# A four-layer selective-scan kernel: y, x and the projection moved in pieces, convolution and input projection in column pairs

## The chip, the cores and the metric

The kernel runs on one core of a Trainium2 chip. The metric is device time in microseconds. A core has TensorE (PE, matmuls, with its weight loads shown apart as PEld), VectorE (DVE), ScalarE (ACT), GpSimd (POOL) and SyncE (SP); each works through its own instructions in order, and semaphores tie them together. In this kernel SP issues every DMA, and sixteen DMA engines carry the data.

## What is computed

Input x is (8, 48, 48, 96): eight images of 48 x 48 positions with 96 channels. Four layers follow each other, each adding to x a two-dimensional selective scan of its group-normalised input. Layers 0 to 2 have dt ranks 6, 16 and 6; layer 3 (rank 6) writes its recurrence as a quotient of cumulative sums.

```python
# one layer; B = 8 images, L = 48*48 positions, Din = 192 channels, N = 16 states, K = 4 directions
xz = gn(x) @ in_proj_w.T
xc, z = split(xz)
u = silu(depthwise_conv3x3(xc) + conv_b)
xs = [rows, columns, rows reversed, columns reversed] of u
dts, Bs, Cs = split(einsum('bkdl,kcd->bkcl', xs, x_proj))
delta = softplus(dt_proj(dts) + dt_bias)
h[n] = exp(delta * A[n]) * h[n] + delta * u * Bs[n]        # along the L positions
y = sum over n of h[n] * Cs[n]  +  D * u                   # summed over the 4 directions
x = x + (layernorm(y) * silu(z)) @ out_proj_w.T
```

## The kernel before

**Tiling.** The eight images are four pairs; a pair (l, p) of layer l is worked through before the next. Its 2 x 192 channels make three tiles t of 128 partitions (tile 0 and 1 the first 128 channels of either image, tile 2 the last 64 of both). For each tile there are two phases ph (along rows, along columns) and two directions d. A position axis of 2304 is cut into three stretches of 768 (`SCANS`); one (t, ph, d, stretch) is a `Chunk` (L684) of 16 scan steps, so a pair has 36 chunks and 576 steps. Step n takes 64 of the tile's 128 channels (n even or odd) and two of the 16 states, one on either half of the partitions, so that it scans 128 x 768 values.

**A scan step.** `load` and `load_b` have SP fetch C (tile cb) and, for six of sixteen steps, B (tile bb), each as two DMAs that broadcast a row of xd in DRAM to 64 partitions (`fetch`, L718 to L729). For the other ten steps TensorE spreads B from the rows in `brow` into PSUM (L667). ScalarE makes the decay exp(delta*A) (L764), GpSimd multiplies bb by du (L741) or VectorE does with the PSUM copy (L794), VectorE scans (L798), GpSimd multiplies cb by the state (L807), and TensorE sums over states into the PSUM tile acc (L854), with 64-column weights, two matmuls side by side.

**The order of work.** `run` (L1170) writes the instructions of the layers out in one order that each engine keeps. Loads for a step are written `LOADS` = 3 steps ahead (B one more), decays 2 ahead, and the sum `LAG` = 2 steps behind. Beside each step stands one step of side work (`beside`, L1264): either of `ahead`, the `prologue` (L287) of the following pair, or of `behind`, the `epilogue` (L998) of the pair before. These are generators; a `yield` ends a step, `yield True` marks that a PSUM bank is held, and `Side(g, total)` carries the number of steps it is expected to have, by which `side_step` keeps the two in proportion. In layer 3, whose chunks are short (`Edge`), ten side steps go beside each scan step. The side work and the preparation of chunks share two PSUM banks (`bank`, L273).

**The prologue.** For each image b of the pair it brings x into SBUF (96 x 2304 fp32, 864 KB): in layer 0 by transposes, and then stores it to the DRAM tile xs (L364); later it loads it from there (L366). Statistics with bn_stats (L373), the group norm, and the input projection to a padded image (L404 for the first 128 channels, L413 for the last 64) follow. `convolve` (L302) sums nine shifted matmuls with diagonal weights into a bank for each of five row groups (`CHUNKS`, four of 480 positions and one of 384). Last come four projections of u (`x_projection`, L467), one for each phase and image: each fills the tile xt, 2*rank + 64 rows by 2304, stores it to xd in DRAM as one DMA (L492; 76 rows, 684 KB, at rank 6, and 96 rows, 864 KB, at rank 16), reads the B rows back (`parts_of`, L431, fetch at L437) and stores them in bf16 parts as xb. `later(i, ...)` places work at step i of a projection's list.

**The sum and the epilogue.** `collect` (L863) copies acc into y, and with a tile's last chunk stores all of y (128 x 2304 fp32, 1152 KB) to yd (L875). The epilogue loads x and y back in pieces of three rows (L1028, 108 KB; L1030, 216 KB), applies layer norm, gate and output projection, and stores the new x (L1104).

Of the kernel before, what the change touches and what calls it, by code (L numbers as in the profile page):

```python
# [49 lines left out]
P = 128  # L50
NB, H, W, DM = 8, 48, 48, 96
L = H * W
# [51 lines left out]
def ss2d_layers_kernel(ctx: ExitStack, tc: tile.TileContext, x_in, consts, weights, out):  # L104
# [178 lines left out]


    GATED, READY = "gated", "ready"

    def prologue(l, p, short=False, first=False):  # L287
        ly = layers[l]
# [13 lines left out]
        def convolve(pad, t):  # L302

            while place["tiles"] < t and not first:
                yield GATED
            u[t] = upool.tile([P, L], F32, name=f"u_{l}_{p}_{t}", tag="u")
            for c0, m in CHUNKS:
                r0, nr = c0 // W, m // W
                ps = bank()
                for j in range(9):  # L310
                    dy, dx = divmod(j, 3)
                    nc.tensor.matmul(  # L312
                        ps[:, :m],
                        ly.diag[:, int(t == 2), j, :],
                        pad[:, r0 + dy : r0 + dy + nr, dx : dx + W],
                        start=(j == 0),
                        stop=(j == 8),
                    )
                    yield True
                nc.scalar.activation(  # L320
                    u[t][:, c0 : c0 + m], ps[:, :m], AF.Identity, bias=ly.column(t, C_CONVB)
                )
                yield
            silu(u[t], u[t])
            yield
# [6 lines left out]
        for b in range(2):  # L332
            x = tmp.tile([DM, L], F32, name=f"x_{l}_{p}_{b}", tag="tmp")
            if l == 0:
                loaded = []

                def load(c0, m):
                    ld = sm2.tile([P, 4, DM], F32, name="ld", tag="ld")
                    nc.sync.dma_start(
                        ld[: m // 4],  # L340
                        x_in[2 * p + b, c0 : c0 + m, :].rearrange("(q j) c -> q j c", j=4),
                    )
                    loaded.append(ld)

                load(*CHUNKS[0])
                load(*CHUNKS[1])
                for _ in range(3):
                    yield
                for i, (c0, m) in enumerate(CHUNKS):
                    q, ld = m // 4, loaded[i]  # L350
                    ps = bank()
                    for j in range(4):
                        nc.tensor.transpose(
                            ps[0:DM, j * q : (j + 1) * q], ld[:q, j, :], ident[:q, :q]
                        )
                    yield True
                    nc.scalar.copy(
                        x[:, c0 : c0 + m].rearrange("c (q j) -> c j q", j=4),
                        ps[0:DM, :m].rearrange("c (j q) -> c j q", j=4),
                    )  # L360
                    if i + 2 < NCH:
                        load(*CHUNKS[i + 2])
                    yield
                nc.sync.dma_start(src[b], x)  # L364
            else:
                nc.sync.dma_start(x, src[b])  # L366
            for _ in range(4):
                yield


            st = sm1.tile([DM, NCH, 6], F32, name="st", tag="st")
            for i, (c0, m) in enumerate(CHUNKS):
                nc.vector.bn_stats(st[:, i, :], x[:, c0 : c0 + m])  # L373
                if i % 2 == 1:
                    yield
            mv = sm1.tile([DM, 2], F32, name="mv", tag="mv")
            nc.vector.bn_aggr(mv, st.rearrange("p a b -> p (a b)"))
            yield
            ps = bank()
            nc.tensor.matmul(ps[0:DM, 0:1], minus_group, mv[:, 0:1], start=True, stop=True)  # L380
            yield True
            mg = sm1.tile([DM, 1], F32, name="mg", tag="mg")
            nc.scalar.copy(mg, ps[0:DM, 0:1])
            dv = sm1.tile([DM, 1], F32, name="dv", tag="dv")
            nc.scalar.activation(dv, mv[:, 0:1], AF.Square, bias=mg)
            nc.scalar.activation(dv, dv, AF.Identity, bias=mv[:, 1:2])
            yield
            ps = bank()
            nc.tensor.matmul(ps[0:DM, 0:1], group_w, dv, start=True, stop=True)
            yield True  # L390
            scale, shift = gn[:, b, 0:1], gn[:, b, 1:2]
            nc.scalar.activation(scale, ps[0:DM, 0:1], AF.Ln, bias=gn_eps[0:DM])
            nc.scalar.activation(scale, scale, AF.Exp, scale=-0.5)
            nc.scalar.activation(shift, mg, AF.Copy, scale=scale)
            nc.scalar.activation(x, x, AF.Identity, bias=shift, scale=scale)
            yield

            pad = padded(f"pad_{l}_{p}_{b}")
            q0 = 64 * b
            for c0, m in CHUNKS:  # L400
                r0, nr = c0 // W, m // W
                rows = slice(1 + r0, 1 + r0 + nr)
                ps = bank()
                nc.tensor.matmul(  # L404
                    ps[:, :m], ly.inw[:, 0:P], x[:, c0 : c0 + m], start=True, stop=True
                )
                yield True
                nc.scalar.copy(
                    pad[:, rows, 1 : W + 1], ps[:, :m].rearrange("p (r w) -> p r w", w=W)
                )  # L410
                yield
                ps = bank()
                nc.tensor.matmul(  # L413
                    ps[q0 : q0 + 64, :m], ly.inw[:, P:DIN], x[:, c0 : c0 + m], start=True, stop=True
                )
                yield True
                nc.scalar.copy(
                    pad2[q0 : q0 + 64, rows, 1 : W + 1],
                    ps[q0 : q0 + 64, :m].rearrange("p (r w) -> p r w", w=W),
                )  # L420
                yield
            if not (first and b == 1):
                yield from convolve(pad, b)
# [43 lines left out]
        def x_projection(i, ph, b):  # L467

            o, got = 15 * i, {}

            def put(ps, c0, m):
                if "xt" not in got:
                    got["xt"] = tmp.tile([ly.nx, L], F32, name=f"xt_{l}_{p}_{ph}_{b}", tag="tmp")
                xt, r0, nr = got["xt"], c0 // W, m // W
                if ph == 0:
                    nc.scalar.copy(xt[:, c0 : c0 + m], ps[: ly.nx, :m])
                else:
                    nc.scalar.copy(
                        xt.rearrange("p (w h) -> p h w", h=H)[:, r0 : r0 + nr, :],
                        ps[: ly.nx, :m].rearrange("p (r w) -> p r w", w=W),  # L480
                    )

            def mul(half, c0, m):
                if half == 0:
                    got["ps"] = bank()
                project(got["ps"], ph, b, half, lambda z: z[:, c0 : c0 + m], slice(0, m))

            for j, (c0, m) in enumerate(CHUNKS):
                later(o + 3 * j, True, mul, 0, c0, m)
                later(o + 3 * j + 1, True, mul, 1, c0, m)  # L490
                later(o + 3 * j + 2, False, lambda *a: put(got["ps"], *a), c0, m)
            later(o + 15, False, lambda: nc.sync.dma_start(xd[ph, b], got["xt"]))  # L492
            row = 2 * ly.rank
            parts_of(
                o + 19, ph, b,
                lambda d: xd[ph, b, row + 2 * NS * d : row + 2 * NS * d + NS, :].rearrange(
                    "n (q m) -> (n q) m", q=4
                ),
                lambda d: xb[ph, b, :, d].rearrange("k n (q m) -> (n q) k m", q=4),
                4 * NS, L // 4,  # L500
            )
# [167 lines left out]
                start=True, stop=True,  # L669
            )  # L670

    late_act, late_sums = [], []

    def collected():
        some = bool(late_sums)
# [8 lines left out]
    class Chunk:  # L684
# [178 lines left out]
        def collect(self):  # L863
# [8 lines left out]
            if self.ph == self.d == 1 and self.last:  # L872
                if t == 0:
                    s["yd"] = dram.tile([3, P, L], F32, name=f"yd_{l}_{p}", tag="yd")
                nc.sync.dma_start(s["yd"][t], s["y", t])  # L875

    class Edge:

# [119 lines left out]
    def epilogue(l, p):  # L998
# [26 lines left out]
        def load(i):  # L1025
# [4 lines left out]
            nc.sync.dma_start(y, yd[:, :, at].rearrange("t p m -> p t m"))  # L1030
            loaded[i] = x, y

        load(0)
        for _ in range(3):
            yield
# [134 lines left out]
    def run(pairs, short):  # L1170
# [58 lines left out]
        for k, ((l, p, unit), c, n) in enumerate(todo):  # L1229
# [4 lines left out]
            per = NS // QUAD if l in short else NS  # L1234
            all_units = len(groups) * (per if l in short else len(SCANS) * per)
            place["tiles"] = 3 * unit // all_units
            if done:
                behind, done = Side(epilogue(*done), 195), None
            if unit == LAG and following:
                ahead = Side(begin(*following), 300)  # L1240
            if k == 0:
                coming_to = 1
                coming = prepare(chunks[coming_to])
# [158 lines left out]
```

## Time and profile before

| | us |
|---|---|
| median of 3 runs | 20514.42 |
| lowest, highest | 20494.02, 20516.52 |
| the profiled execution | 20509.65 |
| its span, first to last instruction | 20507.7 |

Engine busy shares are 84% for TensorE, 86% for VectorE, 79% for ScalarE and 87% for GpSimd. The TensorE clock granted was 0.904 on average. The DMA engines moved 4200 MB, at 217 to 229 GB/s in every full slice of layers 0 to 2, with a busy share near 0.88. Layers 0 to 2 fill the span from 205 us to about 18,565; layer 3 takes the last 1,940 us, in which TensorE is busy for 1,581 and GpSimd for 703.

The DMAs that matter here, from the page's list of issues and the list of DMAs:

| tensors | line | count | KB each |
|---|---|---|---|
| cb<-xd and bb<-xd, the scan's loads | L724 | 13952 and 5184 | 192 |
| brow<-xb | L749, L916 | 864 | 72 |
| yd<-y | L875, and L995 in layer 3 | 48 | 1152 |
| xd<-xt, rank 6 and rank 16 | L492 | 32 and 16 | 684 and 864 |
| x<-xs and xs<-x | L366, L364 | 24 and 8 | 864 |

A group's line gives line, engine, operation, output and inputs with shapes, the count, then busy time and mean duration in ns of one, then the idle time of the engine just before it and what ended most of it. In the timelines the idle time stands in brackets. "SPq" are the queue's own instructions.

### The profile page before, as it was taken

The numbers are of one execution on the slowest core, as the hardware profiler recorded it, in microseconds if no ns is written. First come the engines' busy times: TensorE is split into PE (matmuls) and PEld (weight loads), VectorE is DVE, ScalarE is ACT, GpSimd is POOL, SyncE is SP. The second block draws the span as 40 slices with busy tenths as digits, with TensorE's granted clock in tenths as the row PEclk, the third lists the DMA queues.
The fourth block names the chain that finished last, engine by engine and source line by source line (L and its number), as shares of the span: only waits on it lengthen the run. The fifth ranks groups of instructions, "written<-read, shape, count | busy, mean of one in ns | idle before, by whom it ended". The sixth has DMA issues, their size and how long they took to land. (4 is left out here: it accounts for less than half of the span.)

```text
span 20507.7 us, 304889 instructions
## 1 busy us (share of the span) xinstructions
PE 17283.2 (84%) x88322; PEld 7546.6 (37%) x88322; DVE 17656.0 (86%) x14161; ACT 16243.7 (79%) x30020; POOL 17768.2 (87%) x10121
## 2 busy tenths in 40 slices
PE   8888888888888888888888888888888888888886
PEld 2323333333333333333333333333333333335565
DVE  5999999999999999999999999989989989995543
ACT  5777887887887887887877887877877877877776
POOL 5999999999999999999999999999999999995432
PEclk8998998998998999998998999988988998999997
DMA  5888888888888888888888888888888888883221
GB/s 147 223 221 222 219 220 224 222 219 221 220 225 222 219 229 221 221 229 219 221 228 220 217 225 219 218 218 220 217 219 219 220 219 222 219 220 109 76 72 51
DMA packets 1963444, 4200.13 MB, mean 205 GB/s; under 512 B 369456, under 2 KB 720048, under 8 KB 1948592
## 3 DMA queue, kind: packets, MB, share of 16 engines
q1 hardware_dynamic: 1961776, 4180.52, 77.8%
q8 instruction: 726, 11.89, 0.3%
q14 instruction: 942, 7.72, 0.2%
HBM read 4026.64 MB, written 152.27 MB: 204 GB/s over the span
## 5 line engine op out<-in xcount | busy, mean ns | idle before, releaser
L807 POOL TENSOR_TENSOR cb<-cb,da 128x768 f32<-128x768 f32 x4320 | 7831.3, 1817 | 799.5 <-issue 258.3
L854 PE MATMUL acc<-cb,twin 128*64 128x384 f32 x27648 | 7018.1, 542 | 663.6 <-POOL cb L807 660.3
L798 DVE TENSOR_TENSOR_SCAN da<-da,carry,b 128x768 f32<-128x768 f32 x2880 | 5223.3, 1814 | 176.4 <-ACT b L764 2.3
L741 POOL TENSOR_TENSOR bb<-bb,du 128x768 f32<-128x768 f32 x2592 | 4714.0, 1819 | 361.0 <-DMA bb<-xd 207.8
L794 DVE TENSOR_TENSOR b<-du,b 128x768 f32<-128x768 f32 x4320 | 4087.6, 946 | 883.9 <-PE b L667 785.4
L807 POOL TENSOR_TENSOR cb<-cb,bb 128x768 f32<-128x768 f32 x2592 | 4705.1, 1815 | 155.0 <-DVE bb L798 57.1
L667 PE MATMUL b<-brow,pick 96*64 96x512 bf16 (+2 forms) x18816 | 2761.6, 355 | 1787.6 <-DVE da L798 1408.4
L764 ACT ACTIVATE da<-dl,a 128x768 f32<-128x768 f32 x4320 | 4013.6, 931 | 245.8 <-POOL cb L807 214.0
L854 PEld LDWEIGHTS acc<-cb,twin 128*64 128x64 f32 x27648 | 2268.9, 150 | 3089.4 <-issue 1400.3
L798 DVE TENSOR_TENSOR_SCAN bb<-b,carry,bb 128x768 f32<-128x768 f32 x1728 | 3109.0, 1799 | 114.8 <-ACT b L764 53.5
L764 ACT ACTIVATE b<-dl,a 128x768 f32<-128x768 f32 x2592 | 2334.4, 901 | 590.2 <-DVE da L798 558.4
L798 DVE TENSOR_TENSOR_SCAN da<-da,b 128x768 f32<-128x768 f32 x1440 | 2525.4, 1754 | 85.6 <-DVE b L794 0.9
L667 PEld LDWEIGHTS <-pick 96*64 96x64 bf16 x18816 | 974.1, 114 | 4192.1 <-DVE da L798 2506.3
L578 ACT COPY dl<-ps 64x384 f32<-64x384 f32 x3456 | 1635.3, 473 | 756.7 <-PE ps L623 720.7
L312 PE MATMUL ps<-pad,diag 128*128 128x480 f32 (+1 forms) x4320 | 2165.7, 599 | 11.5 <-DVE eyc L1087 9.9
L623 PE MATMUL ps<-du,cst 128*64 128x384 f32 (+1 forms) x7296 | 1709.7, 516 | 93.1 <-ACT du L617 77.0
L578 ACT COPY du<-ps 64x384 f32<-64x384 f32 x3456 | 1635.7, 473 | 190.0 <-DVE ps L634 91.2
L798 DVE TENSOR_TENSOR_SCAN bb<-b,bb 128x768 f32<-128x768 f32 x864 | 1502.2, 1739 | 94.9 <-ACT b L764 40.5
L623 PE MATMUL ps<-dl,cst 128*64 128x384 f32 (+1 forms) x7296 | 1412.4, 483 | 0.0
L312 PEld LDWEIGHTS ps<-pad,diag 128*128 128x128 f32 x4320 | 687.5, 191 | 1211.4 <-issue 1090.1
L603 PE MATMUL ps<-dts,w 6*128 6x384 f32 (+5 forms) x2432 | 946.3, 595 | 176.1 <-DMA dts<-xd 103.7
L611 ACT ACTIVATE du<-ps,w 128x384 f32<-128x384 f32 (+1 forms) x912 | 521.4, 572 | 622.3 <-PE ps L603 611.5
(144 smaller groups left out, 19159.8 us busy)
## 6 DMA issues: line engine op xcount, KB each, us to landing
cb<-xd SPq DMA_DIRECT2D x13952, 192.0 KB
bb<-xd SPq DMA_DIRECT2D x5184, 192.0 KB
brow<-xb SPq DMA_DIRECT2D x864, 72.0 KB
yd<-y SPq DMA_DIRECT2D x48, 1152.0 KB
ey<-yd SPq DMA_DIRECT2D x256, 216.0 KB
cb<-xd SPq DMA_DIRECT2D x128, 384.0 KB
ex<-xs SPq DMA_DIRECT2D x256, 108.0 KB
xd<-xt SPq DMA_DIRECT2D x32, 684.0 KB
```

The source lines that it names most:

```text
L312: nc.tensor.matmul(ps[:, :m], ly.diag[:, int(t == 2), j, :], pad[:, r0 + dy : r0 + dy + nr, dx : dx + W], start=(j == 0), stop=(j == 8),)
L578: nc.scalar.copy(z[64 * h : 64 * h + 64, g, at], v[64 * g : 64 * g + 64])
L603: nc.tensor.matmul(o[:, :m], ly.dtw[q0 : q0 + r, k, chans], dts[q0 : q0 + r, at], start=True, stop=True,)
L611: nc.scalar.activation(e, v, AF.Abs, bias=bias)
L623: nc.tensor.matmul(v[half], ident[:, half], z1, start=(i == 0), stop=(i == 3))
L667: nc.tensor.matmul(o[64 * h : 64 * h + 64], pick[:, b, n : n + 1].to_broadcast([2 * NR, 64]), rows, start=True, stop=True,)
L741: nc.gpsimd.tensor_mul(b, b, self.du[n % 2])
L764: nc.scalar.activation(da, self.dl[n % 2], AF.Exp, scale=layers[self.l].a2[:, int(self.t == 2), n % 2, k, i : i + 1],)
L794: nc.vector.tensor_mul(b, self.du[n % 2], b)
L798: nc.vector.tensor_tensor_scan(way(h), way(da), way(b), start, ALU.mult, ALU.add)
L807: nc.gpsimd.tensor_mul(c, c, h)
L854: nc.tensor.matmul(self.acc[64 * g : 64 * g + 64, a, : self.m // 2], twin, c[:, a, :], start=False, stop=(pair + 2 == NS and not self.turns),)
```

## The change

```diff
+    halves_of = [slice(64 * g, 64 * g + 64) for g in range(2)]
...
     def convolve(pad, t):
...
-                    nc.tensor.matmul(
-                        ps[:, :m],
-                        ly.diag[:, int(t == 2), j, :],
-                        pad[:, r0 + dy : r0 + dy + nr, dx : dx + W],
-                        start=(j == 0),
-                        stop=(j == 8),
-                    )
+                    for half in halves_of:
+                        nc.tensor.matmul(
+                            ps[half, :m],
+                            ly.diag[:, int(t == 2), j, half],
+                            pad[:, r0 + dy : r0 + dy + nr, dx : dx + W],
+                            start=(j == 0),
+                            stop=(j == 8),
+                        )
                     yield True
...
-                nc.sync.dma_start(src[b], x)
-            else:
-                nc.sync.dma_start(x, src[b])
-            for _ in range(4):
+            for c0, m in CHUNKS:
+                piece = slice(c0, c0 + m)
+                if l == 0:
+                    nc.sync.dma_start(src[b, :, piece], x[:, piece])
+                else:
+                    nc.sync.dma_start(x[:, piece], src[b, :, piece])
+                yield
+            for _ in range(2):
                 yield
...
-                nc.tensor.matmul(
-                    ps[:, :m], ly.inw[:, 0:P], x[:, c0 : c0 + m], start=True, stop=True
-                )
+                for half in halves_of:
+                    nc.tensor.matmul(
+                        ps[half, :m], ly.inw[:, half], x[:, c0 : c0 + m], start=True, stop=True
+                    )
                 yield True
...
-            later(o + 15, False, lambda: nc.sync.dma_start(xd[ph, b], got["xt"]))
+            def store(c0, m):
+                nc.sync.dma_start(xd[ph, b, :, c0 : c0 + m], got["xt"][:, c0 : c0 + m])
+
+            for j, (c0, m) in enumerate(CHUNKS):
+                later(o + 3 * j + 3 if ph == 0 else o + 14 + j // 2, False, store, c0, m)
...
-                o + 19, ph, b,
+                o + 24, ph, b,
...
-    late_act, late_sums = [], []
+    late_act, late_sums, late_stores = [], [], []
+
+    def store_some(n):
+        for _ in range(min(n, len(late_stores))):
+            o, z, at = late_stores.pop(0)
+            nc.sync.dma_start(o[:, at], z[:, at])
...
-                nc.sync.dma_start(s["yd"][t], s["y", t])
+                for z in range(0, L, SCAN // 2):
+                    late_stores.append((s["yd"][t], s["y", t], slice(z, z + SCAN // 2)))
+                if t == 2:
+                    store_some(NS)
...
+        for _ in range(4):
+            yield
         load(0)
...
+            store_some(1)
             if done:
-                behind, done = Side(epilogue(*done), 195), None
+                behind, done = Side(epilogue(*done), 199), None
             if unit == LAG and following:
-                ahead = Side(begin(*following), 300)
+                ahead = Side(begin(*following), 311)
```

Each convolution matmul, and each of L404, becomes two with 64 columns of weights, one for either half of the output's partitions. x, y and xt are moved in pieces: x and xt in the five row groups of `CHUNKS` (180 KB of x, 143 or 180 KB of xt, the last of each smaller), y in six pieces of 192 KB, which wait in a list from which each scan step takes one; with the last tile they all go out at once. In phase 0 a piece of xt follows its copy by one step, in phase 1, where every copy writes all over xt, five pieces go out in three steps from the last copy on. Reading back begins five steps later than before, the epilogue's first load four steps later, and the two totals follow. In layer 3 y is stored by other code, which stays.

## The prediction

> **What bounds the kernel now.** I read the page's totals first, then the costliest groups, then sums over chosen stretches, then the timelines of single stalls.
>
> ```profile
> PE 17283.2 (84%) x88322; PEld 7546.6 (37%) x88322; DVE 17656.0 (86%) x14161; ACT 16243.7 (79%) x30020; POOL 17768.2 (87%) x10121
> ...
> L807 POOL TENSOR_TENSOR cb<-cb,da 128x768 f32<-128x768 f32 x4320 | 7831.3, 1817 | 799.5 <-issue 258.3
> ...
> L741 POOL TENSOR_TENSOR bb<-bb,du 128x768 f32<-128x768 f32 x2592 | 4714.0, 1819 | 361.0 <-DMA bb<-xd 207.8
> ...
> L807 POOL TENSOR_TENSOR cb<-cb,bb 128x768 f32<-128x768 f32 x2592 | 4705.1, 1815 | 155.0 <-DVE bb L798 57.1
> ```
>
> Four engines stand near 85%, so the share alone decides nothing. Layers 0 to 2 are 12 pairs of 576 scan steps, 6912 in all. The first scan begins at 205 us and the last ends at about 18,562: 2.656 us a step, 42.5 us a chunk of 16. GpSimd must make 16 products at L807 and 6 at L741 in a chunk: 22 x 1.818 = 40.0 us. That is the floor. A chunk is 2.5 us above it, 432 chunks 1,080 us; of this some 125 us is other GpSimd work (the subtractions at L445 and L452). So about 950 us of stalls is all that any edit can win there. Next, where they lie (columns: length, busy time of each engine, granted clock, DMA share, GB/s):
>
> ```profile
> 13456.00:13577.00 121.00, 115.15 (x534) 38.93 (x532) 113.86 (x85) 91.06 (x172) 117.30 (x67) 0.99 0.90 228
> 13655.00:13846.00 191.00, 151.71 (x664) 52.37 (x662) 155.67 (x114) 132.01 (x235) 167.52 (x97) 0.84 0.83 219
> 7539.00:7716.00 177.00, 144.06 (x663) 50.98 (x664) 154.53 (x113) 132.13 (x237) 167.20 (x97) 0.89 0.89 238
> ```
>
> Row one is three chunks that hold nothing but scan and convolution, at 40.3 us a chunk: TensorE is at 95% and GpSimd still at 97%. Rows two and three are the same four chunks of two pairs, in which the four projections are stored: 191 us in a layer of rank 6, 177 in the layer of rank 16, with equal GpSimd work. In the slow one the DMA moves less, not more.
>
> What a large transfer does, in the chain of waits and on GpSimd:
>
> ```profile
> 13634.56 11.05 DMA cb<-xd
> ...
> 13646.13 0.75 SPq L749
> ...
> 13646.92 6.21 DMA brow<-xb
> ```
>
> ```profile
> 12441.67 1.83 POOL L807 TENSOR_TENSOR cb<-cb,da 128x768 f32<-128x768 f32 x1
> 12449.64 1.80 POOL L741 TENSOR_TENSOR bb<-bb,du 128x768 f32<-128x768 f32 x1 [6.14 <-DMA bb<-xd]
> ```
>
> The first load issued after the projection's store (L492, at 13633.5) takes 11 us, where one in an ordinary stretch takes 4.65 (bb, at 12069.9). Only then does the queue go on to brow, for which TensorE waits. In the second, y (1152 KB at 12431.7) and x (864 KB at 12439.5) precede a stall of 6.1 us.
>
> **What the Trainium skill says.** "DMA: Bandwidth & Descriptors", section "Why a DMA increments its semaphore by 16 and not by 1": a transfer is spread over the largest number of engines up to 16 that divides its slowest dimension. The projection has 76 rows in layers of rank 6, hence 4 engines, and 96 in the layer of rank 16, hence 16. The trace agrees: loads behind it reach 11 us in the first kind alone, and after each of these stores four late completions are counted instead of sixteen. "TensorEngine Tiling (Array Packing)", section "Key Properties": tiles of columns run in parallel, and a change of tiling mode drains the array. The trace agrees with both, next part.
>
> **The change, part by part.** Sums are against the profiled execution, 20,509.65 us (span 20,507.7); the median of the runs shown is 4.8 us above it.
>
> (a) *Column pairs on TensorE.* In the stretch at 13,456 a convolution matmul (two instructions, 480 columns) stands alone between 64-column ones: 13460.57 to 13461.57, 1.00 us. In a row they cost 7.25 us for 18 (18,784.5), 0.403 each, 0.81 a matmul. A matmul after an L854 group starts 0.74 us behind it (13461.92 to 13462.66); an L413, itself 64 columns wide, 0.65 (5008.05 to 5008.70). So the mode costs 0.2 us at the end and 0.1 at the start. A pair of 384 columns takes 0.64 (eight L623 instructions, end to end 1.29, are two); for 480 columns 0.80. Twice the instructions, the same array time, 0.3 us less per isolated matmul. Some 1,665 convolution matmuls lie among scan steps, and 130 of L404: 1,795 x 0.3 = 540 us off TensorE. What is it worth? In row one, where TensorE is fullest, GpSimd loses under 1 us a chunk: nothing there. In chunks 2 to 24 of a pair, which mix convolution and epilogue, the scans' starts stand 50 us a pair above the floor, 600 in twelve pairs; there TensorE would catch up faster after a stall. The bounds are 0 and half, 300. I take 50, since what stops TensorE there is often one of the two PSUM banks that ScalarE and VectorE have yet to empty (3.11 us ahead of L404 at 12,952, ended by eyc at L1087), and pairs leave that alone. In layer 3 and at the start convolution runs in a row, at the same price: 0.
>
> (b) *The projection, 48 stores in 240 pieces.* Same rows, so still 4 engines in rank 6. The four-engine form costs (191 - 177)/4 = 3.5 us a store more; 32 of these, 110 us. In phase 0 a piece goes out with every third step, which leaves the four engines time between; in phase 1 five go in three steps, a little better than one. I take 55 of 110, bounds 0 and 110. At the start the store overlaps the projection: 5.
>
> (c) *x, 24 loads and 8 stores in pieces.* Stalls of 6.1 us (above) and of 1.5 + 0.9 (12,820) by a load: about 4 us each, 19 in layers 1 to 2 and for layer 3's first: 76. In layer 3 five more, where VectorE waits 3.55 for x at 18,634 and the chain holds 7.93 and 7.22 us of it. Pieces let the loads pass in between, and statistics begin on the first piece. I take 50 + 15, bounds 20 and 100.
>
> (d) *y.* Pieces one a step for two of three tiles, the third all at once. The stalls at y alone are small: row one begins with the store of a pair's second tile (13,456) and shows none. I take 20, bounds 0 and 60. The four empty steps ahead of the epilogue's first load spare SP its 40.5 us of waiting for y at L1030, in 16 places: 15.
>
> (e) *Costs.* 180 + 192 + 128 more DMAs, 0.35 to 0.6 us of SP each: 250 us on a queue that works 60% of the time (20,900 issues at 0.55) and mostly waits for buffers (2,222 us on L854). Cover: the loads' lead of three steps, 8 us. Prologue 300 to 311 steps and epilogue 195 to 199: 510 in a pair that offers some 540, so still done in time. GpSimd, VectorE and ScalarE work is unchanged.
>
> Sum: 50 + 60 + 65 + 35 = 210. 20,510 - 210 = 20,300; with the 5 us to the median, 20,305, told as 20,300.
>
> **Rivals.**
> 1. *Both count*: TensorE's 540 us are worth half of the mixed chunks' stalls (300), and the transfers give 270. For it: 84% busy, and PE in-order behind scan waits. Against: row one. 20,510 - 570 = 19,940; from 20,120 down is its ground.
> 2. *Hidden anyway*: the same bytes on the same engines; the stall only spreads, and new steps shift the order of banks. For it: y at unit 388 costs nothing today. 20,460, between 20,420 and 20,550.
> 3. *Slower: SP loses its lead.* A piece must wait on SP for the ScalarE copy just before it, five times a projection instead of once, and the trace counts eight completion semaphores used in turn, so five pieces take five of eight places. Behind each wait stand the loads for three steps on. It decides once a wait exceeds 8 - 5 = 3 us (lead less a load's time). If each of the 240 pieces then costs 1.5 us, 360, less 150 gained: 20,720. Against: SP reaches the store early and a step's copy comes at most a step, 2.7 us, later.
> That a pair doesn't overlap its halves is excluded by L623 and L854, whose pairs share one bank and, at L623, one moving operand.
>
> **How the numbers follow.** Forecast (20,120 to 20,420) 0.52, rival 1 0.18, rival 2 0.19, rival 3 0.11. Range 20,000 to 20,500. A measurement of this kernel can tell 0.2%, 41 us. Faster than that takes the forecast, rival 1 and half of rival 2: 0.80; within it 0.10; slower 0.10. The likeliest case's own range is 20,120 to 20,420.
>
> **What would show it.** (a) L312 at 64 columns, 8,640 instructions, each pair 0.80 us apart, TensorE's busy time down by about 500 us, row one unchanged in length. (b) No load of 11 us behind L492 and the rank 6 stretch nearer 177 us. (c) no 6 us gap on GpSimd near unit 7 of a pair. Wrong: DMA waits of GpSimd as before, or SP waiting on ScalarE's xt for hundreds of us.

## The result, and the profile after

| | before | after |
|---|---|---|
| median (four runs each), us | 20504.22 | 20212.72 |
| lowest, highest | 20487.45, 20516.52 | 20178.94, 20225.01 |
| the profiled execution | 20509.65 | 20200.44 |
| its span | 20507.7 | 20198.6 |
| granted TensorE clock, mean | 0.904 | 0.908 |

The ratio of the times is 0.9852, with a 95% interval of 0.9841 to 0.9864: 303 us less, in a range of 279 to 326. The prediction was 20,300. The page of the changed kernel has these lines (group lines: count, then busy time and mean ns, then idle time before):

```profile
PE 16790.8 (83%) x92962; PEld 7792.6 (39%) x92962; DVE 17667.0 (87%) x14161; ACT 16224.6 (80%) x30014; POOL 17769.4 (88%) x10121
...
L823 POOL TENSOR_TENSOR cb<-cb,da 128x768 f32<-128x768 f32 x4320 | 7835.9, 1819 | 749.3 <-issue 253.1
...
L757 POOL TENSOR_TENSOR bb<-bb,du 128x768 f32<-128x768 f32 x2592 | 4716.9, 1820 | 222.2 <-DMA bb<-xd 125.6
L823 POOL TENSOR_TENSOR cb<-cb,bb 128x768 f32<-128x768 f32 x2592 | 4706.8, 1816 | 100.2 <-DVE bb L814 50.7
...
L314 PE MATMUL ps<-pad,diag 128*64 128x480 f32 (+1 forms) x8640 | 2339.7, 567 | 34.6 <-ACT du L589 24.4
```

VectorE's, ScalarE's and GpSimd's work is as before to 0.2%. TensorE lost 492 us. GpSimd's idle time ahead of its three product groups fell from 799.5 + 361.0 + 155.0 = 1315.5 to 1071.7 us, by 244; the largest part, 139, is that ahead of the bb products, which wait for a load. The same three stretches, summed over windows of the changed kernel (length; busy time of PE, PEld, DVE, ACT, POOL; granted clock; DMA share; GB/s):

```profile
13252.00:13372.00 120.00, 108.08 (x632) 48.82 (x630) 113.81 (x85) 93.76 (x176) 117.47 (x67) 0.97 0.89 232
13454.00:13635.00 181.00, 149.25 (x678) 53.07 (x676) 155.41 (x114) 132.69 (x235) 166.14 (x96) 0.86 0.83 225
7425.00:7596.00 171.00, 144.51 (x674) 53.35 (x675) 154.93 (x113) 132.62 (x235) 164.19 (x95) 0.90 0.91 237
```

The convolution stretch shrank from 121 to 120 us although TensorE has 7 us less to do in it; the two projection stretches went from 191 to 181 and from 177 to 171. In these two pairs the changed rank 6 stretch still needs 10 us more than the rank 16 one; over all pairs the difference is 1.3, as the table below has it.

Taking the first scan of each chunk on VectorE as a clock splits every kernel's span into three: what lies ahead of the first scan, layers 0 to 2 from first to last scan, and the rest, nearly all layer 3. The last two columns are chunks 29 to 32 of a pair, in which the projections are stored, as a mean over the eight pairs of rank 6 and the four of rank 16. The differences are against the one profiled execution of the kernel before, so a row is good to some 20 us; the profiled execution of s1_epi lies 27 us above the median of its runs, that of c_inproj 22 below. The intervals stand with the experiments.

| profiled execution of | first scan at | layers 0-2 | after the last scan | rank 6 | rank 16 |
|---|---|---|---|---|---|
| the kernel before | 205.0 | 18354.8 | 1948.0 | 182.1 | 174.8 |
| the changed kernel | 177.5 (-27) | -237 | -45 | 173.1 | 171.8 |
| e1_pairs | 180.9 (-24) | -76 | -11 | 181.1 | 175.1 |
| c_inproj | 185.7 (-19) | -32 | -4 | 181.1 | 175.1 |
| e2_pieces | 194.7 (-10) | -128 | -45 | 173.7 | 169.3 |
| e3_shift | 205.1 (0) | -97 | -42 | 176.0 | 174.2 |
| s3_fetch | 207.2 (+2) | -76 | -15 | 175.0 | 169.9 |
| s1_epi | 205.8 (+1) | +22 | -40 | 180.3 | 173.9 |
| s4_idle | 205.2 (0) | +17 | -32 | 179.6 | 175.4 |
| e4_rows | 202.6 (-2) | -120 | +8 | 171.1 | 174.6 |
| e6_x | 202.9 (-2) | -75 | +21 | 178.7 | 177.5 |
| e7_y | 206.3 (+1) | -9 | +5 | 181.8 | 175.6 |
| f1_rows | 183.4 (-22) | -313 | -45 | 170.7 | 168.8 |
| f2_piecerows | 173.6 (-31) | -269 | -44 | 172.6 | 169.6 |

### The profile page after: what moved, and what is told of

Its sections match the earlier page's. It is cut to its first block, busy times and chain, and to the rows that moved or that the text cites. A ratio compares the mean times of both kernels' runs of the same rounds, so it can differ in the third digit from the quotient of the medians.

```text
span 20198.6 us, 314848 instructions
## 1 busy us (share of the span) xinstructions
PE 16790.8 (83%) x92962; PEld 7792.6 (39%) x92962; DVE 17667.0 (87%) x14161; ACT 16224.6 (80%) x30014; POOL 17769.4 (88%) x10121
## 4 chain that ended last, share of the span: by engine, by line
PE 21%; ACT 17%; DVE 14%; DMA 10%; issue 9%; POOL 3%; SPq 2%; DVEq 0%; POOLq 0%; ACTq 0%
DVE da L814 7%; PE acc L870 5%; PE ps L634 4%; DMA bb<-xd 4%; DVE b L810 4%; DMA cb<-xd 4%; ACT b L780 3%; ACT dl L589 3%; PE ps L314 2%; PE b L678 2%; ACT du L589 2%; POOL cb L823 2%; DVE bb L814 2%; ACT da L780 2%; SPq L740 1%
## 5 line engine op out<-in xcount | busy, mean ns | idle before, releaser
L870 PE MATMUL acc<-cb,twin 128*64 128x384 f32 x27648 | 7200.8, 539 | 721.3 <-POOL cb L823 704.5
L814 DVE TENSOR_TENSOR_SCAN da<-da,carry,b 128x768 f32<-128x768 f32 x2880 | 5223.2, 1814 | 176.0 <-DVE b L810 0.9
L678 PE MATMUL b<-brow,pick 96*64 96x512 bf16 (+2 forms) x18816 | 2852.5, 353 | 1886.2 <-DVE da L814 1528.4
L870 PEld LDWEIGHTS acc<-cb,twin 128*64 128x64 f32 x27648 | 2452.5, 149 | 2998.4 <-POOL cb L823 1333.5
L678 PEld LDWEIGHTS <-pick 96*64 96x64 bf16 x18816 | 1077.9, 115 | 4164.4 <-DVE da L814 2717.6
L314 PE MATMUL ps<-pad,diag 128*64 128x480 f32 (+1 forms) x8640 | 2339.7, 567 | 34.6 <-ACT du L589 24.4
L634 PE MATMUL ps<-dl,cst 128*64 128x384 f32 (+1 forms) x7296 | 1485.2, 483 | 0.0
L614 PE MATMUL ps<-dts,w 6*128 6x384 f32 (+5 forms) x2432 | 961.4, 605 | 205.0 <-DMA dts<-xd 105.4
L314 PEld LDWEIGHTS ps<-pad,diag 128*64 128x64 f32 x8640 | 751.8, 139 | 885.0 <-issue 729.6
```

What stands on the lines that cost most here:

```text
L314: nc.tensor.matmul(ps[half, :m], ly.diag[:, int(t == 2), j, half], pad[:, r0 + dy : r0 + dy + nr, dx : dx + W], start=(j == 0), stop=(j == 8),
L614: nc.tensor.matmul(o[:, :m], ly.dtw[q0 : q0 + r, k, chans], dts[q0 : q0 + r, at], start=True, stop=True,)
L634: nc.tensor.matmul(v[half], ident[:, half], z1, start=(i == 0), stop=(i == 3))
L678: nc.tensor.matmul(o[64 * h : 64 * h + 64], pick[:, b, n : n + 1].to_broadcast([2 * NR, 64]), rows, start=True, stop=True,)
L814: nc.vector.tensor_tensor_scan(way(h), way(da), way(b), start, ALU.mult, ALU.add)
L870: nc.tensor.matmul(self.acc[64 * g : 64 * g + 64, a, : self.m // 2], twin, c[:, a, :], start=False, stop=(pair + 2 == NS and not self.turns),)
```

## The experiments

Each is an edit of the kernel before, unless it says otherwise. A ratio is against runs of the kernel before on the same chip.

### First: the parts apart

**e1_pairs**: the two column-pair edits alone.

```diff
-                        ps[:, :m],
-                        ly.diag[:, int(t == 2), j, :],
+                    for half in halves_of:
...
+                            ps[half, :m],
+                            ly.diag[:, int(t == 2), j, half],
...
-                    ps[:, :m], ly.inw[:, 0:P], x[:, c0 : c0 + m], start=True, stop=True
+                for half in halves_of:
...
+                        ps[half, :m], ly.inw[:, half], x[:, c0 : c0 + m], start=True, stop=True
```

> Column pairs alone, every transfer as before. If the transfers brought the gain, as predicted: 50 us under the kernel before (20 to 80), TensorE's busy time down by some 500 us all the same, GpSimd's waits for bb and cb as before. If TensorE's freed time counted: 150 to 300 us under it, won in the chunks that mix convolution and epilogue.

Measured: 20399.69 against 20510.05 us, ratio 0.9953 (0.994 to 0.9966): 96 us by the ratio, 110 by the medians. That is twice the 50 that the prediction gave to the pairs, and it lies between the two cases that the expectation named. From its page:

```profile
PE 16886.9 (83%) x92962; PEld 7841.0 (38%) x92962; DVE 17650.3 (87%) x14161; ACT 16238.7 (80%) x30020; POOL 17773.3 (87%) x10121
```

The pairs alone take 17283.2 - 16886.9 = 396 us off TensorE's busy time (at a mean granted clock of 0.900, against 0.904), so a quarter of it shows in the time.

**e2_pieces**: all the rest of the change, with the full-width matmuls; against the changed kernel it is the diff of e1_pairs turned round:

```diff
-                    for half in halves_of:
...
-                            ly.diag[:, int(t == 2), j, half],
+                        ly.diag[:, int(t == 2), j, :],
```

> All transfers in pieces, with the later loads and the new totals; convolution and input projection in full width. If the transfers brought the gain: 160 to 240 us under the kernel before, and with the pairs' gain it adds up to the change's 290. If TensorE's freed time counted: 50 to 130 us under.

Measured: 20316.2 us, ratio 0.9906 (0.9892 to 0.992): 193 us. With the 96 to 110 of e1_pairs the two make 289 to 304; the whole change measures 291.5 by the medians and 303 by the ratio. The parts add up, so within these intervals TensorE's slack and the transfers don't feed on the same stalls.

**e3_shift**: whole transfers, but every step that the change moves is moved.

```diff
-            for _ in range(4):
+            for _ in range(7):
                 yield
...
-                o + 19, ph, b,
+                o + 24, ph, b,
...
+        for _ in range(4):
+            yield
         load(0)
...
-                behind, done = Side(epilogue(*done), 195), None
+                behind, done = Side(epilogue(*done), 199), None
...
-                ahead = Side(begin(*following), 300)
+                ahead = Side(begin(*following), 311)
```

> Only the steps are shifted (three more empty steps after each x, reading back five steps later, the epilogue's first load four later, the new totals); every transfer is whole, convolution in full width. If the pieces themselves act: within 40 us of the kernel before. If loads some steps behind their stores, or the new order of side steps, are what counts: 60 to 150 us under it.

Measured: 20381.63 us, ratio 0.994 (0.9928 to 0.9952): 123 to 128 us without one transfer cut. About two thirds of what e2_pieces gains is the shift of steps; cutting adds 65 (20381.63 to 20316.2). This the prediction had nearly the other way round, with 15 for steps and 145 for pieces.

**e4_rows**: the rank 6 projection still goes out at once and by all columns, but as 64 rows and 12 rows.

```diff
-            later(o + 15, False, lambda: nc.sync.dma_start(xd[ph, b], got["xt"]))
+            def store():
+                for r in ([slice(0, ly.nx)] if ly.nx % 16 == 0 else [slice(0, 64), slice(64, ly.nx)]):
+                    nc.sync.dma_start(xd[ph, b, r], got["xt"][r])
+
+            later(o + 15, False, store)
```

> The kernel before with one edit: at rank 6 the store of the projection is two DMAs, 64 rows and 12 rows, so that the bulk can run on sixteen engines instead of four. If the four engines make the 11 us behind a store: no load of 11 us behind it any more, the rank 6 stretch as short as the rank 16 one (3.5 us a store), 60 to 110 us under the kernel before. If the size of the transfer makes it: within 30 us of the kernel before.

Measured: 20409.82 us, ratio 0.9949 (0.9936 to 0.9961): 100 to 105 us, for 32 more DMAs in 20 ms. Its windows over the same three stretches:

```profile
13373.00:13494.00 121.00, 115.23 (x547) 40.65 (x545) 113.64 (x85) 92.09 (x172) 116.03 (x67) 0.99 0.86 229
13576.00:13752.00 176.00, 145.30 (x666) 50.36 (x666) 154.56 (x113) 132.16 (x236) 166.78 (x97) 0.87 0.87 234
7487.00:7665.00 178.00, 147.85 (x658) 51.95 (x658) 154.05 (x113) 132.16 (x235) 166.62 (x97) 0.85 0.87 236
```

The rank 6 stretch falls from 191 to 176, the other two stand where they stood. The table says it for all pairs: chunks 29 to 32 lose 11.0 us a pair in rank 6 (88 us in eight pairs) and 0.2 in rank 16. The 64 rows split evenly over sixteen engines and the 12 over twelve, by what the Trainium skill states in "DMA: Bandwidth & Descriptors", section "Why a DMA increments its semaphore by 16 and not by 1" (as many engines, up to 16, as divide the slowest dimension). The prediction took 4 engines for 76 rows from there; this run, which changes the rows of a transfer and nothing else, bears it out in time. The records of the single DMA packets bear it out directly: in the kernel before, the last of a rank 6 store's 76 packets (9216 bytes, one a row) ends 10.0 us after the store's issue (median of 32 stores), with five or six of them under way at the most; in e4_rows it ends after 5.4 us, with 16 to 19 under way at the most. In the chain of waits of the whole kernel before, 14 DMAs take over 10 us; the longest in that of e4_rows takes 8.0.

### Second: which of the moved steps

**s3_fetch**: only the reading back of the B rows, five steps later.

```diff
-                o + 19, ph, b,
+                o + 24, ph, b,
...
-                ahead = Side(begin(*following), 300)
+                ahead = Side(begin(*following), 305)
```

> The kernel before with the reading back of the projection five steps later, the total 305, the store still whole. If the read waits on its store's landing and holds up SP: 30 to 70 us under the kernel before, in chunks 28 to 32 of the rank 6 layers. If the read was late enough already: within 25 us of it.

Measured: 20404.29 against 20503.26 us, ratio 0.995 (0.9938 to 0.9962): 99 to 103 us, most of e3_shift and more than either case of its expectation. The argument of `parts_of` moves all that follows the store, ScalarE's cast of what is read as well as the read. The waits of the kernel before point at the place (engine, tile and line that waited; for what; us in total, times, longest):

```profile
POOL bb L741 <- DMA bb<-xd: 207.8, 97, 16.0
...
PE b L667 <- DMA brow<-xb: 178.9, 50, 8.6
...
ACT parts L441 <- DMA raw<-xd: 131.2, 34, 11.5
```

and those of s3_fetch:

```profile
POOL bb L741 <- DMA bb<-xd: 145.0, 84, 6.4
...
PE b L667 <- DMA brow<-xb: 107.0, 33, 5.7
...
ACT parts L441 <- DMA raw<-xd: 11.5, 1, 11.5
```

"raw" is what is read back. ScalarE's cast of it (L441) stands in ScalarE's own order, ahead of the decays of the next scan steps. One such wait in the kernel before, on ScalarE's timeline (start, us, instruction, idle time before in brackets):

```profile
12108.37 0.19 ACT L682 COPY carry<-da 128x1 f32<-128x1 f32 x1 [0.16 <-DVE da L798]
12113.87 0.67 ACT L441 CAST parts<-raw 128x576 bf16<-128x576 f32 x1 [5.31 <-DMA raw<-xd]
12114.45 0.93 ACT L764 ACTIVATE da<-dl,a 128x768 f32<-128x768 f32 x1
```

The decay da at 12114.45 needs nothing of raw; it is held up for 5.3 us with it. SP's timeline has the store and the read:

```profile
12091.40 0.43 SPq L492 DMA_DIRECT2D xd<-xt  x1
...
12106.55 1.23 SPq L437 DMA_DIRECT2D raw<-xd  x2
```

It isn't the store that is waited for, though the expectation had it so. The read goes out 15 us after the store, whose last packet ended at 12101.0; at all 48 reads of these layers' projections the store's last packet has ended before the read is issued, and SP waits ahead of a read for the store in one place only, 7.9 us, in both kernels.

What is short is the way from the read to its use: in the kernel before ScalarE comes to the cast 4.4 us after the read is issued (median of the 51 reads that fall among the scans), and the read's packets take some 5.6; in s3_fetch it comes after 10.3, and 33 of the 34 waits are gone. Read and cast were both moved by five steps, so the distance in steps is as before. But 39 of 51 reads before are issued in the last three steps of a chunk, where SP also has dts and brow of the next chunk to issue, and in s3_fetch 34 of 51 in a chunk's third or fourth step. That this makes the way longer is likely, but no run moves the read without the cast, nor changes the total to 305 without moving them.

The four chunks with the projections lose 57 us in rank 6 and 20 in rank 16, so the gain needs no four-engine store. The waits for bb and brow fall with the one for raw, and GpSimd's wait L741 for cb rises, from 55.0 to 89.2; so the gain isn't ScalarE's alone, and the runs don't split the 99 us.

**s1_epi**: only the epilogue's first load four steps later. **s4_idle**: the control, the same four empty steps and total, but behind that load.

```diff
+        for _ in range(4):
+            yield
         load(0)
...
-                behind, done = Side(epilogue(*done), 195), None
+                behind, done = Side(epilogue(*done), 199), None
```

```diff
         load(0)
-        for _ in range(3):
+        for _ in range(7):
             yield
```

> The kernel before with four empty steps ahead of the epilogue's first load, and its total 199. If the shift's 128 us come from loads that no longer wait on the store just before them: 40 to 90 us under the kernel before, with SP's 40 us at the y load gone and most of the 42 us that the shift won after layer 2. If they come from the later reading back or from x's steps: within 25 us of it.

> A control for the order alone: the kernel before with four more empty steps after the epilogue's first load, not ahead of it, and its total 199. If s1_epi's 37 us came from loading y later: within 20 us of the kernel before. If any new proportion of the side steps brings as much: 20 to 60 us to either side.

Measured: s1_epi 20466.03 against 20503.26, ratio 0.9982 (0.9975 to 0.9989), 37 us, which is between the two cases of its expectation; s4_idle 20498.0 against 20513.33, ratio 0.9992 (0.9984 to 1.0001), which is no change at its interval's edge. The intervals overlap, so that the later load is what pays is likely and not shown. Both gain behind the last scan (-40 and -32 in the table); that they lose some 20 in layers 0 to 2 is within what a row is good for. In s4_idle SP's wait for y at L1030 stays, 36.9 us where it was 40.5, and in s1_epi it is 12.6: what s4_idle gains in layer 3 can't come from that wait. The control says something on s3_fetch too: in s4_idle the wait for raw fell to 59.7 us as well, with 15 us of time. So the total of a wait isn't a price list; what the list did rightly was to point at the place.

### Third: the other pieces, and the input projection

**c_inproj**: of e1_pairs only L404. **e6_x**: only the pieces of x, with a total of 306. **e7_y**: only those of y.

```diff
-                    ps[:, :m], ly.inw[:, 0:P], x[:, c0 : c0 + m], start=True, stop=True
+                for half in halves_of:
...
+                        ps[half, :m], ly.inw[:, half], x[:, c0 : c0 + m], start=True, stop=True
```

```diff
-                nc.sync.dma_start(src[b], x)
-            else:
-                nc.sync.dma_start(x, src[b])
-            for _ in range(4):
+            for c0, m in CHUNKS:
+                piece = slice(c0, c0 + m)
...
+                    nc.sync.dma_start(x[:, piece], src[b, :, piece])
+                yield
+            for _ in range(2):
                 yield
```

```diff
-                nc.sync.dma_start(s["yd"][t], s["y", t])
+                for z in range(0, L, SCAN // 2):
+                    late_stores.append((s["yd"][t], s["y", t], slice(z, z + SCAN // 2)))
...
```

> The kernel before with column pairs in the input projection alone (L404), convolution in full width. If the 24 us that the pairs won before the first scan come from the input projection no longer changing the mode of the array at each matmul, with the clock granted sooner: first scan near 181 us instead of 205, 20 to 45 us in all. If they come from the convolution: first scan at 205, under 20 us in all.

> The kernel before with x alone in pieces and its total 306. If loads behind a whole x are what stalled, as predicted: 50 to 80 us under the kernel before, and no 6 us gap at the start of a pair. If the read-back of the projection and the epilogue's load were what counted: within 30 us.

> The kernel before with y alone in pieces. Predicted: 20 us under the kernel before (0 to 60). If y's size never mattered: within 20 us.

Measured, against 20513.33: c_inproj 20476.85, ratio 0.9981 (0.9974 to 0.9988), 37 us; e6_x 20445.77, ratio 0.9963 (0.9949 to 0.9977), 68 to 76 us; e7_y 20510.7, ratio 1.0 (0.9992 to 1.0009), nothing. In e6_x ScalarE's wait for raw is 46.5 us too, since x's two further steps shift what follows; so its 68 us aren't purely x's. Counted by chunks, as in the table, e6_x loses 41 us in chunks 1 to 10 of the pairs, where x is loaded, and 59 in chunks 23 to 32, where it isn't; and e3_shift, with x whole and its later steps, loses 37 in chunks 1 to 10. So it isn't shown that cutting x gains anything beyond the steps that come with it. The pieces of xt alone weren't tried.

### Last: rows instead of pieces

**f1_rows**: the changed kernel, with its five pieces of xt replaced by the store of e4_rows (reading back stays at o + 24). **f2_piecerows**: the changed kernel, with each piece cut into 64 and 12 rows. Both diffs are against the changed kernel; rows is the list of row slices of e4_rows.

```diff
-            for j, (c0, m) in enumerate(CHUNKS):
-                later(o + 3 * j + 3 if ph == 0 else o + 14 + j // 2, False, store, c0, m)
+            later(o + 15, False, store)
```

```diff
             def store(c0, m):
-                nc.sync.dma_start(xd[ph, b, :, c0 : c0 + m], got["xt"][:, c0 : c0 + m])
+                for r in rows:
+                    nc.sync.dma_start(xd[ph, b, r, c0 : c0 + m], got["xt"][r, c0 : c0 + m])
```

> The kernel after, but the projection's store is whole again, one step after its last copy, at rank 6 as two DMAs of 64 and 12 rows. If what remains in the chunks of the projection is the four engines' load: 30 to 80 us under the kernel after. If the pieces already took what was to be had: within 25 us of it. If size matters and not the engines: 30 to 60 us over it.

> The kernel after, with each piece of the projection at rank 6 split into 64 and 12 rows. If the four engines' load is what remains: 40 to 90 us under the kernel after, better than whole rows where pieces help too. If the doubled number of DMAs takes their places among the eight: 0 to 40 us over the whole-row form.

Measured against 20503.26: f1_rows 20132.6 (20113.64 to 20141.6), ratio 0.9819 (0.9807 to 0.9832); f2_piecerows 20169.89 (20162.93 to 20195.0), ratio 0.9843 (0.983 to 0.9856). f1_rows beats the changed kernel, whose interval begins at 0.9841, by some 70 us. Windows of f1_rows:

```profile
13212.00:13332.00 120.00, 107.63 (x632) 48.63 (x630) 113.46 (x84) 93.76 (x176) 117.09 (x67) 0.97 0.88 233
13416.00:13586.00 170.00, 145.95 (x684) 49.82 (x683) 155.34 (x114) 132.97 (x237) 164.76 (x96) 0.90 0.90 237
7398.00:7568.00 170.00, 145.65 (x680) 52.76 (x680) 155.16 (x114) 132.69 (x236) 164.51 (x96) 0.91 0.89 241
```

In these two pairs rank 6 and rank 16 now take the same 170 us. Over all pairs the change is smaller: the table has 173.1 and 171.8 for the changed kernel, 170.7 and 168.8 for f1_rows. So rank 6, where the rows are divided, loses 2.4 us a pair, and rank 16, where five pieces only become one store again, 3.0. These chunks hold 31 of the 76 us by which f1_rows is shorter in layers 0 to 2; where the rest comes from isn't shown. What pieces do in the slower of the two pairs can be read in the chain of waits of the changed kernel, over the stretch of 181 us (start, us, piece; the DMAs alone):

```profile
13486.42 6.97 DMA brow<-xb
...
13526.63 6.82 DMA xd<-xt
...
13535.45 6.47 DMA brow<-xb
...
13585.93 6.70 DMA bb<-xd
13592.64 4.45 DMA cb<-xd
```

A piece of 143 KB on four engines is itself in the chain, with 6.8 us, and three of the four loads take 6.5 to 7 us. In f1_rows the chain over the same work, in its 170 us, holds just two DMAs:

```profile
13470.80 3.35 DMA bb<-xd
...
13573.83 3.24 DMA cb<-xd
```

The waits of the two kernels agree. The changed kernel:

```profile
PE b L678 <- DMA brow<-xb: 154.9, 45, 5.9
...
POOL bb L757 <- DMA bb<-xd: 125.6, 107, 4.0
```

and f1_rows:

```profile
PE b L680 <- DMA brow<-xb: 95.3, 33, 5.3
...
POOL bb L759 <- DMA bb<-xd: 74.4, 64, 4.8
```

The longest wait for bb falls from 16.0 us to 4.0 in the changed kernel, but that is not the pieces' doing, for e3_shift, with whole transfers, has nearly the same:

```profile
POOL bb L741 <- DMA bb<-xd: 118.9, 90, 4.6
```

TensorE's wait for brow stays nearly as it was in the changed kernel (178.9 before). f2_piecerows, with pieces and rows both, isn't told apart from the changed kernel by its interval, and none of its five runs reaches down to the slowest of f1_rows. So of the projection's edits the cutting by columns isn't what pays: once the rows divide well and reading back comes later, two stores by rows at the end do better than ten small ones. Whether that is for their number or for when they go out is open, and a whole store of 76 rows in the changed kernel wasn't tried.

## Why the prediction was right, and where its sum was not

The forecast was 210 us less time, the runs gave 291.5 to 303, within the range and in the likeliest case's own. The mechanisms named were there, except that of y; the pairs, the start and the epilogue were set too low, the pieces of y and of the projection too high, and a term of 99 us, as large as any, was missing. That the sum landed in its range all the same is partly luck: the missing term alone is more than the 82 to 93 us by which the forecast fell short, and terms set too high made up for others set too low.

**(a) The pairs: 50 predicted, 96 to 110 measured, bounds 0 to 300.** The price was right. On TensorE's timeline in the changed kernel (start, us, instruction; x4 is one pair, of two instructions a half):

```profile
13266.17 0.97 PE L314 MATMUL ps<-pad,diag 128*64 128x480 f32 x4
13266.97 0.49 PE L678 MATMUL b<-brow,pick 96*64 96x512 bf16 x4
13267.30 0.81 PE L870 MATMUL acc<-cb,twin 128*64 128x384 f32 x4
```

The pair begins at 13266.17 and what follows it at 13266.97: 0.80 us, where the full-width matmul held 1.00 and 0.1 more ahead of it. 540 us were to come off TensorE; 396 did in e1_pairs, 492 in the whole change. The worth in scans was set at 50 and is 76, spread thinly over the mixed chunks; row one, "nothing there", gave 1 us of 121. 24 us more lie ahead of the first scan and 11 behind the last, to both of which the step "at the start convolution runs in a row, at the same price: 0" gave nothing. For the start that step failed: c_inproj, the pairs of the input projection alone, brings 19 of the 24, with a clock that rises sooner, below. Of the 300 us that rival 1 gave the pairs the runs leave 96 to 110.

**(b) The projection: 55 + 5 predicted.** The cost of the four-engine form, 110, was about right: e4_rows takes away 100 to 105. But the way to it, a rank 16 pair as measure of a rank 6 one, was weaker than it looked: the two windows shown differ by 14 us, the means over all pairs by 7.3 (182.1 and 174.8), likely since a rank 16 store is larger and pays for that. Rank 6 with divided rows comes out below rank 16 (171.1 and 174.6). The pieces were given half of the 110; that was too much, for rank 6 stood at 176.0 with the shift alone and at 173.7 with the pieces (8 x 2.3 = 18 us), and the chain above suggests why: a piece on four engines is short, but still on four engines. In rank 16, where the pieces change no engines, the same two kernels differ by more (174.2 and 169.3).

The missing term is the reading back five steps later. The prediction put it under costs, "still done in time", at 0; s3_fetch shows 99 to 103. The line was in the list of waits of before, 131.2 us for raw, and wasn't weighed.

**(c) x: 50 + 15 predicted, 68 to 76 measured** in e6_x, with the reservation told there: the size came out, the mechanism isn't shown. The gap of 6.1 us on GpSimd near unit 7 of a pair, which the prediction showed, is 1.5 in the changed kernel at this place:

```profile
12272.31 1.81 POOL L823 TENSOR_TENSOR cb<-cb,da 128x768 f32<-128x768 f32 x1
12275.58 1.81 POOL L757 TENSOR_TENSOR bb<-bb,du 128x768 f32<-128x768 f32 x1 [1.46 <-DMA cb<-xd]
```

Pieces of x aren't needed for that. GpSimd's longest wait in steps 5 to 20 of a pair, over the eleven pairs that follow another, is 7.0 us in the kernel before and 3.7 in the changed one, but also 4.5 in e3_shift and 4.1 in s1_epi, which leave x whole and only part it from the other transfers by some steps.

**(d) y: 20 predicted, nothing measured** (between 16 us less and 18 more by its interval). The evidence that the prediction itself gave, no stall at y in row one, pointed there. The epilogue's later load: 15 predicted, 37 measured (15 in the control). SP's wait for y fell from 40.5 us in 16 places to 12.8 in 4, but the gain lies in layer 3, which the prediction hadn't looked at for it, and the control gains most of it without that fall.

**(e) Costs.** The new DMAs cost nothing that a run shows. SP's waits for ScalarE's xt at the piece stores come to 79.0 us (58.0 of it one wait) and 46.4, not to hundreds. The 58.0 us stand before the first scan, where the kernel before has 79.4 at its store. Among the scan steps the point from which rival 3 decides, a wait over 3 us on SP with loads behind it, is passed in two places, with 4.1 us and 3.0, too few to weigh. Rival 2, the stall that only spreads, falls with the result itself, 20,213 against its 20,420 and more; its remark that new steps shift the order was worth more than the prediction made of it, for by e3_shift the steps are the larger part of what the transfers gain.

Still open: what x's later steps are worth alone (128 of e3_shift less 99 and 37 leaves about nothing, the count by chunks some 37), how much of s3_fetch is ScalarE's and how much the loads', what beside the rows makes f1_rows faster, and the pieces of xt without the shift.

## What to carry to other kernels

Before a transfer is cut by size, see over how many engines its rows divide: 64 + 12 rows instead of 76 won 100 us, more than the 65 that cutting x, y and the projection into pieces adds to the later steps. Look in the list of waits for an engine in order that waits for a small thing read back from DRAM: what stands behind it pays. Then see in the queue's timeline when the read is issued and when its user comes to it. Moving the read and its use by a few steps can be worth as much as any other part of a change, so a moved step is never costed at nothing for being "in time". And measure one stage against another over all its repetitions, not by one pair of them.

## What the runs showed of the hardware that wasn't expected

**The clock at the start.** TensorE's granted clock in the kernel before is 0.55 from 83 to 120 us, where the input projection runs. Full-width matmuls there alternate with 64-column ones, and TensorE's timeline shows no gap from 99.61 on:

```profile
99.61 1.97 PE L404 MATMUL ps<-x,w 96*128 96x480 f32 x2 [4.08 <-ACT x L395]
101.51 1.86 PE L413 MATMUL ps<-x,w 96*64 96x480 f32 x2
103.30 1.97 PE L404 MATMUL ps<-x,w 96*128 96x480 f32 x2
...
115.95 1.54 PE L413 MATMUL ps<-x,w 96*64 96x384 f32 x2
```

In e1_pairs, where all are 64 columns wide, the same work:

```profile
91.75 1.87 PE L407 MATMUL ps<-x,w 96*64 96x480 f32 x4 [4.08 <-ACT x L397]
93.41 1.81 PE L416 MATMUL ps<-x,w 96*64 96x480 f32 x2
94.33 1.91 PE L407 MATMUL ps<-x,w 96*64 96x480 f32 x4
96.08 0.97 PE L416 MATMUL ps<-x,w 96*64 96x480 f32 x2
96.89 1.03 PE L407 MATMUL ps<-x,w 96*64 96x480 f32 x4
```

The first stays at 1.9 us a matmul for 18 us; in the second the same L416 halves from 1.81 to 0.97 some 4 us after the start, and the input projection ends after 10 us instead of 18. The first image shows the same: 28.21 to 46.02 us before, 28.73 to 39.50 in e1_pairs (the trace's records of the granted clock begin later, at 48.9 and 34.1 us). c_inproj, which changes L404 alone, shows the same halving (1.96 at 94.20, 1.03 at 96.81) and 19 us off the first scan. The Trainium skill, "TensorE: Matmul & The Clock Gate", section "What's actually happening", says that the clock goes up after about 3.4 us of sustained work; the second trace agrees, the first does not. Full width alone isn't what holds the clock down: in the kernel before it is 0.50 from 99 to 120 us and 1.00 from 121 on, some 3 us into the row of full-width convolution matmuls that begins at 117.42. That the alternation of widths holds the clock down is what the two traces suggest; that it does so by itself, apart from the gaps that a change of width may leave in the array, no run here shows.

**A read issued too close ahead of its use costs the engine that uses it.** Casts of 0.67 us on ScalarE, an engine 79% busy, held up what stood behind them for 131 us in 34 places, 5.3 us at the one shown, though the stores ahead of the reads had landed; all but 11.5 us of it went when read and cast moved by five steps.
